# A GNN layer's edge sums: two masked sums per partition on VectorE in place of eight bf16 matmuls on TensorE

## The chip, the cores and the metric

The kernel runs on one core of one Trainium2 chip. The core has five engines that run on their own and meet at semaphores: TensorE (PE, matrix products), VectorE (DVE), ScalarE (ACT), GpSimd (POOL, which here issues the gathers) and SyncE (SP, which here issues loads and stores). SBUF is the working memory of 128 partitions; matrix products land in PSUM. The metric is the device time of one execution in microseconds (us), as a median of several runs.

## What is computed

One layer of a graph network with 6250 nodes, 206250 edges and 64 features. The edges are sorted by destination node `dst`; every node has one loop edge and on average 33 edges.

```python
h = jnp.maximum(_layernorm(x, axis=-1), 0.0)

def _L0_gnn_ref(x, edge_index, edge_attr, W1, b1, W2, b2):
    src = edge_index[0]
    dst = edge_index[1]
    msg = jax.nn.relu(x[src] + edge_attr)
    agg = jax.ops.segment_sum(msg, dst, num_segments=x.shape[0])
    h = x + agg
    h = jax.nn.relu(h @ W1 + b1)
    return h @ W2 + b2

x = x + _L0_gnn_ref(h, edge_index, edge_attr_64, ...)
```

So: normalise the node rows, gather one row per edge, add the edge's own row, relu, sum per destination node, then two 64x64 layers.

## The kernel before

**Tiling.** The edges go in `NG` = 201 groups of 1024 (`GE`: 128 partitions with `G` = 8 consecutive edges each) and a tail group of 426 edges in `CT` = 4 columns. Nodes go in `NB` = 12 blocks of 512 and a rest of 106. Since the edges are sorted, a group touches a window of consecutive nodes; the kernel sums each group into a window of `W` = 64 nodes that begins at the group's first node.

**Start** (lines 72 to 226). Node rows are loaded, normalised (`ln_head`, `ln_rows`), written to DRAM as `h_rows` for the gathers, and turned by TensorE (`ln_turn`; ScalarE copies them) into `z`, which holds the sums, one column per node. The first `RAW` = 4 groups gather raw `x` rows, since `h_rows` isn't written yet, and are normalised per edge (`norm_edges`). Then `slot` is made: for each edge the place of its node in its group's window, from `base`, the window starts, which a one-row matmul spreads over the partitions (lines 214 to 226).

**The edge loop** (lines 342 to 355), for each group g:
- `load` (134): SP loads the edge rows `ea`, and POOL issues eight indirect DMAs (130), one for each column of 128 rows, into `xg`. Both have `LOOK` = 12 buffers, so POOL may be up to 12 groups ahead of the instruction that reads a buffer last.
- `window_sum` (287): a one-hot `oh` of `slot` against `wslots`, which lies in PSUM (294); `full = xg + ea` into PSUM (299); relu and a split of the fp32 messages into three bf16 parts, ScalarE and VectorE by turns (301 to 305); eight matmuls that add the three parts of all edges into `agg`, 64 nodes by 3 x 64 (308).
- `turn(g-1)` (275): VectorE adds the three parts of the group before into `agg_rows` (278), and TensorE transposes them (280).
- `sum_into_z(g-2)` (283): VectorE adds the transpose into `z` at a column read from a register (285). `LAG` = 2 is this distance.
- `blocks_behind(g-2)` (335): once all edges of a block of nodes are in (`READY`), `hidden` (312) makes relu(W1 z + b1), and at the next group `result` (321) makes the second product, adds `x` and stores.

At g = 8, `find_left` (239) marks edges that no window holds, and `flag`; at g = 9, `b2` is added to `x_sb` by 13 additions (353, 355). After the loop a register reads `flag`; if any edge is left, a second loop over all groups and windows repairs the result (379 to 399). With these inputs it has nothing to do.

**Order.** The schedule is written out by hand: each engine takes its instructions in the order of the program, and waits in it. POOL and SP wait for nothing but buffers and, at the stores, for SP's data, so they run ahead of the others.

Of the kernel before, what the change touches and what calls it, by code (L numbers as in the profile page):

```python
# [18 lines left out]
P = 128  # L19
G = 8  # L20
GE = P * G
# [15 lines left out]
LOOK = 12  # L37
LAG = 2
RV = 8
RAW = 4  # L40
# [5 lines left out]
def kernel(  # L46
# [143 lines left out]
    def ln_turn(c, h):  # L190
        for b in range(XC if c < NB else 1):
            pt = psum.tile([D, R, P], F32, name="big", bufs=1)
            n0 = (c + b) * P * R
            if c < NB:
                for r in range(R):
                    nc.tensor.transpose(pt[:, r, :], h[:, b * R + r, :], ident)  # L196
                nc.scalar.copy(z[:, n0:n0 + P * R].rearrange("d (p r) -> d r p", r=R), pt)  # L197
            else:
                nc.tensor.transpose(pt[:, 0, :TN], h[:TN, 0, :], ident[:TN, :TN])
                nc.scalar.copy(z[:, n0:N], pt[:, 0, :TN])  # L200

    heads, rows = [], []
# [6 lines left out]
    rows.append(ln_rows(*heads[-1]))  # L209
    ln_turn(*rows[-2])  # L210
# [3 lines left out]
    base = const.tile([1, NG + 1], F32, name="base")  # L214
    nc.vector.tensor_copy(base, dst_sb[0:1, 0:C + 1:G])
    pb = psum.tile([P, R * D], F32, name="out", bufs=1)
    nc.tensor.matmul(pb[:, :NG + 1], ones[0:1, :], base, start=True, stop=True)
# [10 lines left out]

    def combine(xg, ea, n):
        nc.vector.tensor_tensor(xg[:, :n], xg[:, :n], ea[:, :n], ALU.add)  # L230
        msg = work.tile([P, G, D], F32, name="msg")
        nc.scalar.activation(msg[:, :n], xg[:, :n], AF.Relu)
        return msg
# [3 lines left out]
    flag = const.tile([1, 1], I32, name="flag")  # L237

    def find_left():
        nc.vector.tensor_scalar(left, slot, 1.0, None, op0=ALU.is_lt)  # L240
        nc.vector.scalar_tensor_tensor(left, slot, float(W), left, op0=ALU.is_gt, op1=ALU.add)
# [5 lines left out]
        nc.tensor.matmul(pf[0:1, 0:1], most, ones[:, 0:1], start=True, stop=True)  # L247

# [23 lines left out]

    turned = {}

    def turn(g):
        pa = aggs.pop(g)
        rows = work.tile([W, D], F32, name="agg_rows")
        nc.vector.tensor_reduce(rows, pa.rearrange("w t d -> w d t"), AX.X, ALU.add)  # L278
        pt = psum.tile([D, W], F32, name="turned", bufs=1)
        nc.tensor.transpose(pt, rows, ident[:W, :W])  # L280
        turned[g] = pt

    def sum_into_z(g):
        at = window_start(g)
        nc.vector.tensor_tensor(z[:, ds(at, W)], z[:, ds(at, W)], turned.pop(g), ALU.add)  # L285

    def window_sum(g):
        n = G if g < NG else CT
        cols = cols_of(g)
        ea, xg = loaded[g] if g < RAW else load(g)  # L290
        if g < RAW:
            norm_edges(xg)
        oh = work.tile([P, G, W], BF16, name="oh")
        nc.vector.tensor_tensor(  # L294
            oh[:, :n], slot[:, cols].unsqueeze(2).to_broadcast([P, n, W]),
            wslots.unsqueeze(1).to_broadcast([P, n, W]), ALU.is_equal)

        full = psum.tile([P, G, D], F32, name="full", bufs=2)
        nc.vector.tensor_tensor(full[:, :n], xg[:, :n], ea[:, :n], ALU.add)  # L299
        parts = work.tile([P, G, 3, D], BF16, name="parts")  # L300
        nc.scalar.activation(parts[:, :n, 0, :], full[:, :n], AF.Relu)  # L301
        nc.vector.scalar_tensor_tensor(full[:, :n], full[:, :n], 0.0, parts[:, :n, 0, :],  # L302
                                       op0=ALU.max, op1=ALU.subtract)
        nc.scalar.copy(parts[:, :n, 1, :], full[:, :n])  # L304
        nc.vector.tensor_tensor(parts[:, :n, 2, :], full[:, :n], parts[:, :n, 1, :], ALU.subtract)  # L305
        pa = psum.tile([W, 3, D], F32, name="agg", bufs=2)
        for j in range(n):
            nc.tensor.matmul(pa, oh[:, j, :], parts[:, j], start=(j == 0), stop=(j == n - 1))  # L308
        aggs[g] = pa


    def hidden(c):
        n0 = c * P * R
        p, r = (P, R) if c < NB else (TN, 1)
        p1 = psum.tile([D, P * R], F32, name="big", bufs=1)
# [5 lines left out]
    def result(c, h1):  # L321
# [3 lines left out]
        for k in range(r):  # L325
            nc.tensor.matmul(p2[:p, k * D:(k + 1) * D], h1[:, k, :p], w2_sb, start=True, stop=True)  # L326
        o = work.tile([P, R, D], F32, name="o")
# [5 lines left out]
    hid = {}  # L333

    def blocks_behind(g):
        for c in sorted(hid):
            result(c, hid.pop(c))
        for c in range(NB):
            if READY[c] == g:
                hid[c] = hidden(c)  # L340

    for g in range(NG + 1):
        window_sum(g)
        if g >= 1:
            turn(g - 1)
# [5 lines left out]
        if g == 9:  # L351
# [4 lines left out]
    sum_into_z(NG + 1 - LAG)  # L356
    blocks_behind(NG + 1 - LAG)
    turn(NG)
    for g in range(NG + 2 - LAG, NG + 1):
        sum_into_z(g)  # L360
        blocks_behind(g)
    hid[NB] = hidden(NB)
    for c in sorted(hid):
        result(c, hid.pop(c))


    def all_windows(msg, lf, n):
        for w in range(0, N, WB):
# [3 lines left out]
            pw = psum.tile([D, WB], F32, name="big", bufs=1)  # L372
# [7 lines left out]
    with tc.If(any_left > 0):  # L380
# [17 lines left out]
        for c in range(NB + 1):  # L398
            result(c, hidden(c))
# [39 lines left out]
```

## Time and profile before

| | us |
|---|---|
| median of 6 runs | 2361.32 |
| lowest, highest | 2356.5, 2387.14 |
| the profiled execution, timed | 2357.45 |
| its span in the profile | 2355.7 |
| POOL busy, 1612 gathers | 1589.7 |
| first gather starts, last one ends | 4.6, 2287.1 |
| VectorE busy | 668.8 |
| TensorE busy (ends modelled) | 414.0 |
| ScalarE busy | 267.9 |

The page gives busy time of each engine, a chain of waits followed back from the end, and groups of instructions with the line of the kernel: so many, their busy time, the mean of one in ns, the idle time of the engine before them and what ended it ("issue": nothing that the profile shows; "remote": a semaphore whose setter isn't known). The timeline lists instructions in order of time: start in us, duration, engine, line, and in brackets the idle time before. Durations of one group's instructions on VectorE: L294 0.67, L299 0.69, L302 0.70, L305 0.69, L278 0.34, L285 0.21 us.

### The profile page before, as it was taken

The page shows a single profiled execution, that of the slowest core. Times are in us where ns is not written, and L with a number is a line of the kernel's source. Part 1 is how long each engine was busy: PE and PEld are TensorE (multiplying, and loading weights), DVE is VectorE, ACT ScalarE, POOL GpSimd, SP SyncE. Part 2 cuts the span into 40 slices and gives each one's busy share as a digit, 9 for nine tenths or more (in the row PEclk, how much of TensorE's full clock was granted, in tenths as well). Part 3 has the DMA queues.
Part 4 walks back from the last instruction along what each step waited for, and adds up shares of the span by engine and source line. Part 5 has one row for each costly group of instructions (what it writes and reads, how often), then busy time and mean ns, then how long its engine had stood idle before and what let it go on. Part 6 is the DMA issues. An engine that isn't in the chain of part 4 may idle for free.

```text
span 2355.7 us, 9645 instructions
## 1 busy us (share of the span) xinstructions
PE 414.0 (18%) x1991; PEld 287.0 (12%) x1991; DVE 668.8 (28%) x1321; ACT 267.9 (11%) x450; POOL 1590.9 (68%) x1619
## 2 busy tenths in 40 slices
PE   1101320031122012030122013001212011120303
PEld 1000210020011011020111012001111011110202
DVE  3313621141242133150243124112324023131515
ACT  2100210010011011020011011001111011010202
POOL 7775777567667757577567757766666676766760
DMA  5111131012113103111203103110311130130310
GB/s 160 39 35 35 28 94 31 21 45 76 26 22 99 26 19 94 30 24 51 69 23 94 35 19 94 31 23 21 92 32 23 24 96 21 26 98 21 91 23 4
DMA packets 87525, 112.95 MB, mean 48 GB/s; under 512 B 30948, under 2 KB 35684, under 8 KB 87460
## 3 DMA queue, kind: packets, MB, share of 16 engines
q0 software_dynamic: 51584, 52.93, 10.0%
q1 hardware_dynamic: 34628, 57.65, 7.3%
q10 hardware_dynamic: 1248, 1.70, 0.2%
q14 instruction: 48, 0.39, 0.1%
q8 instruction: 17, 0.28, 0.0%
HBM read 108.96 MB, written 3.20 MB: 48 GB/s over the span
## 4 chain that ended last, share of the span: by engine, by line
another core or an unknown queue 33%; issue 31%; DVE 13%; POOL 11%; ACT 5%; DVEq 3%; DMA 2%; PE 2%; ACTq 0%; SPq 0%; POOLq 0%
POOL xg L130 11%; DVE full L302 4%; DVE full L299 3%; ACT parts L301 3%; ACT parts L304 2%; DVE parts L305 2%; DVE oh L294 2%; DVEq L265 2%; DMA xg<-h_rows,src_sb 1%; DVEq L299 1%; PE agg L308 1%; DVE agg_rows L278 1%; DVE z L285 1%; DMA x_sb<-in_x_dram 0%
## 5 line engine op out<-in xcount | busy, mean ns | idle before, releaser
L130 POOL DMA_INDIRECT xg<-h_rows,src_sb x1580 | 1557.2, 986 | 683.3 <-issue 456.3
L308 PE MATMUL agg<-parts,oh 128*64 128x192 bf16 x1612 | 299.7, 367 | 903.9 <-DVE parts L305 504.8
L308 PEld LDWEIGHTS <-oh 128*64 128x64 bf16 x1612 | 229.8, 167 | 958.3 <-DVE parts L305 543.9
L301 ACT ACTIVATE parts<-full 128x512 bf16<-128x512 f32 x202 | 120.2, 595 | 1696.7 <-DVE full L299 1254.6
L278 DVE TENSOR_REDUCE agg_rows<-agg 64x64 f32<-64x192 f32 x202 | 69.4, 343 | 825.6 <-remote 669.4
L280 PE MATMUL turned<-ident,agg_rows 64*64 64x64 f32 x202 | 63.1, 312 | 962.3 <-issue 493.4
L302 DVE SCALAR_TENSOR_TENSOR full<-full,parts 128x512 f32<-128x512 f32 x202 | 141.1, 699 | 229.1 <-ACT parts L301 109.8
L305 DVE TENSOR_TENSOR parts<-full,parts 128x512 bf16<-128x512 f32 x202 | 139.4, 690 | 131.5 <-ACT parts L304 83.9
L299 DVE TENSOR_TENSOR full<-xg,ea 128x512 f32<-128x512 f32 x202 | 138.5, 686 | 64.7 <-DMA ea<-in_edge_attr_dram 31.1
L280 PEld LDWEIGHTS turned<-ident,agg_rows 64*64 64x64 f32 x202 | 25.4, 126 | 1024.4 <-issue 538.4
L304 ACT CAST parts<-full 128x512 bf16<-128x512 f32 x202 | 118.2, 585 | 154.6 <-DVE full L302 113.2
L294 DVE TENSOR_TENSOR oh<-slot,wslots 128x512 bf16<-128x512 f32 x202 | 135.7, 672 | 0.0
L285 DVE TENSOR_TENSOR z<-z,turned 64x64 f32 x202 | 42.0, 208 | 227.6 <-remote 131.9
L328 DVE TENSOR_TENSOR o<-out,x_sb 128x256 f32<-128x256 f32 (+1 forms) x13 | 5.3, 410 | 127.3 <-remote 62.2
L130 POOL DMA_INDIRECT xg<-in_x_dram,src_sb x32 | 32.6, 1017 | 12.3 <-issue 9.5
L316 PE MATMUL big<-z,w_sb 64*64 64x512 f32 (+1 forms) x26 | 24.2, 1032 | 0.3 <-DVE z L285 0.3
L326 PE MATMUL out<-w_sb,h 64*128 64x64 f32 (+1 forms) x98 | 23.6, 418 | 1.2 <-ACT h L318 1.2
L326 PEld LDWEIGHTS out<-w_sb,h 64*128 64x128 f32 (+1 forms) x98 | 22.3, 329 | 3.2 <-ACT h L318 3.2
L318 ACT ACTIVATE h<-big,b_sb 64x512 f32<-64x512 f32 (+1 forms) x13 | 8.5, 656 | 123.3 <-issue 48.1
L196 PE MATMUL big<-ident,ln_h 128*64 128x128 f32 x48 | 12.7, 420 | 52.6 <-issue 21.0
L197 ACT COPY z<-big 64x512 f32<-64x512 f32 x12 | 12.6, 1050 | 39.7 <-issue 30.6
L196 PEld LDWEIGHTS big<-ident,ln_h 128*64 128x64 f32 x48 | 6.4, 158 | 58.5 <-issue 41.7
(52 smaller groups left out, 64.2 us busy)
## 6 DMA issues: line engine op xcount, KB each, us to landing
ea<-in_edge_attr_dram SPq DMA_DIRECT2D x201, 256.0 KB
xg<-h_rows,src_sb POOLq DMA_INDIRECT x1580
x_sb<-in_x_dram SPq DMA_DIRECT2D x4, 384.0 KB
h_rows<-ln_h SPq DMA_DIRECT2D x4, 384.0 KB
out_dram<-o SPq DMA_DIRECT2D x12, 128.0 KB
dst_sb<-in_dst_main_dram ACTq DMA_DIRECT2D x1, 804.0 KB
src_sb<-in_src_main_dram ACTq DMA_DIRECT2D x1, 788.0 KB
xg<-in_x_dram,src_sb POOLq DMA_INDIRECT x32
```

The lines of the kernel that those rows point to most:

```text
L130: nc.gpsimd.indirect_dma_start(out=xg[:, j, :], out_offset=None, in_=rows[:, :], in_offset=bass.IndirectOffsetOnAxis(ap=idx[:, j:j + 1], a ...
L265: _, vals = nc.values_load_multi_w_load_instructions(dst_sb[0:1, g * G:(g + n - 1) * G + 1:G], engines=(DVE,), min_val=0, max_val=N - 1)
L278: nc.vector.tensor_reduce(rows, pa.rearrange("w t d -> w d t"), AX.X, ALU.add)
L280: nc.tensor.transpose(pt, rows, ident[:W, :W])
L285: nc.vector.tensor_tensor(z[:, ds(at, W)], z[:, ds(at, W)], turned.pop(g), ALU.add)
L294: nc.vector.tensor_tensor(oh[:, :n], slot[:, cols].unsqueeze(2).to_broadcast([P, n, W]), wslots.unsqueeze(1).to_broadcast([P, n, W]), ALU. ...
L299: nc.vector.tensor_tensor(full[:, :n], xg[:, :n], ea[:, :n], ALU.add)
L301: nc.scalar.activation(parts[:, :n, 0, :], full[:, :n], AF.Relu)
L302: nc.vector.scalar_tensor_tensor(full[:, :n], full[:, :n], 0.0, parts[:, :n, 0, :], op0=ALU.max, op1=ALU.subtract)
L304: nc.scalar.copy(parts[:, :n, 1, :], full[:, :n])
L305: nc.vector.tensor_tensor(parts[:, :n, 2, :], full[:, :n], parts[:, :n, 1, :], ALU.subtract)
L308: nc.tensor.matmul(pa, oh[:, j, :], parts[:, j], start=(j == 0), stop=(j == n - 1))
```

## The change

Within a partition, the eight consecutive edges of a group belong to at most two nodes here, a first and a last one. `cut` makes, once, two masks of all edges: `of_run[0]`, equal to the partition's first slot, and `of_run[1]`, equal to its last slot but not its first; `run_slot` keeps the two slots (a third for the tail's fourth column). For each group, VectorE then adds `ea` to `xg` in place in SBUF, and for each mask takes max(., 0) times the mask into `msg` and sums its eight edges into a column block of `sums`, 128 x 64 fp32. TensorE multiplies `sums` with a one-hot of the partition's slots, now fp32, made for `OB` = 4 groups at a time: two fp32 matmuls a group, which give node columns directly, so `agg_rows`, the transpose and the split are gone. ScalarE has no part in it any more.

The sum into `z` follows six groups behind (`LAG`), the buffers are 14 (`LOOK`), five groups gather raw rows (`RAW`), the window starts are spread before the last two `ln_turn`, the flag is judged at g = 14, `b2` is added at g = 15, and a block's second product and its store come two and four groups after its first product. An edge in a third node of its partition would count as left.

```diff
+RUNS = 2
-LOOK = 12
-LAG = 2
+LOOK = 14
+LAG = 6
+OB = 4
-RAW = 4
+RAW = 5
...
+    def cut(g, n, cols, k):
+        sv = slot[:, cols].rearrange("p (g j) -> p g j", j=k)
+        first, last = [t[:, cols].rearrange("p (g j) -> p g j", j=k) for t in of_run]
+        nc.vector.tensor_tensor(first, sv, sv[:, :, 0:1].to_broadcast([P, n, k]), ALU.is_equal)
+        nc.vector.tensor_tensor(last, sv, sv[:, :, k - 1:k].to_broadcast([P, n, k]), ALU.is_equal)
+        nc.vector.tensor_tensor(last, last, first, ALU.is_gt)
+        nc.vector.tensor_copy(run_slot[:, g:g + n, 0], sv[:, :, 0])
+        nc.vector.tensor_copy(run_slot[:, g:g + n, 1], sv[:, :, k - 1])
+    cut(0, NG, slice(0, C), G)
+    cut(NG, 1, slice(C, C + TJ), TJ)
...
     def find_left():
-        nc.vector.tensor_scalar(left, slot, 1.0, None, op0=ALU.is_lt)
-        nc.vector.scalar_tensor_tensor(left, slot, float(W), left, op0=ALU.is_gt, op1=ALU.add)
+        nc.vector.tensor_tensor(left, of_run[0], of_run[1], ALU.add)
+        nc.vector.tensor_scalar(left, left, 0.5, None, op0=ALU.is_lt)
+        nc.vector.scalar_tensor_tensor(left, slot, 1.0, left, op0=ALU.is_lt, op1=ALU.max)
+        nc.vector.scalar_tensor_tensor(left, slot, float(W), left, op0=ALU.is_gt, op1=ALU.max)
         nc.vector.scalar_tensor_tensor(left, dst_sb, 1.0, left, op0=ALU.add, op1=ALU.mult)
...
     def sum_into_z(g):
         at = window_start(g)
-        nc.vector.tensor_tensor(z[:, ds(at, W)], z[:, ds(at, W)], turned.pop(g), ALU.add)
+        nc.vector.tensor_tensor(z[:, ds(at, W)], z[:, ds(at, W)], aggs.pop(g), ALU.add)
+    def one_hot(g, n, runs):
+        oh = work.tile([P, OB, RUNS + 1, W], F32, name="oh", bufs=4)
+        nc.vector.tensor_tensor(
+            oh[:, :n, :runs], run_slot[:, g:g + n, :runs].unsqueeze(3).to_broadcast([P, n, runs, W]),
+            wslots.unsqueeze(1).unsqueeze(1).to_broadcast([P, n, runs, W]), ALU.is_equal)
...
     def window_sum(g):
-        nc.vector.tensor_tensor(full[:, :n], xg[:, :n], ea[:, :n], ALU.add)
-        ...
-        for j in range(n):
-            nc.tensor.matmul(pa, oh[:, j, :], parts[:, j], start=(j == 0), stop=(j == n - 1))
+        sums = work.tile([P, RUNS + 1, D], F32, name="sums", bufs=LAG + 2)
+        nc.vector.tensor_tensor(xg[:, :m], xg[:, :m], ea[:, :m], ALU.add)
+        for k in range(RUNS):
+            msg = work.tile([P, G, D], F32, name="msg")
+            nc.vector.scalar_tensor_tensor(
+                msg[:, :n], xg[:, :n], 0.0, of_run[k][:, col:col + n].unsqueeze(2).to_broadcast([P, n, D]),
+                op0=ALU.max, op1=ALU.mult)
+            nc.vector.tensor_reduce(sums[:, k], msg[:, :n].rearrange("p j d -> p d j"), AX.X, ALU.add)
+        ...
+        for k in range(runs):
+            nc.tensor.matmul(pa, sums[:, k], oh[:, k], start=(k == 0), stop=(k == runs - 1))
...
     def blocks_behind(g):
+        for c in sorted(res):
+            if READY[c] + 4 <= g:
+                store(c, res.pop(c))
         for c in sorted(hid):
-            result(c, hid.pop(c))
+            if READY[c] + 2 <= g and not res:
+                res[c] = result(c, hid.pop(c))
```

## The prediction

> **What bounds the kernel now.** I read the costliest groups first, then the list of waits, then three stretches of the timeline. The page's busy times and the shares of its chain:
>
> ```profile
> PE 414.0 (18%) x1991; PEld 287.0 (12%) x1991; DVE 668.8 (28%) x1321; ACT 267.9 (11%) x450; POOL 1590.9 (68%) x1619
> ...
> another core or an unknown queue 33%; issue 31%; DVE 13%; POOL 11%; ACT 5%; DVEq 3%; DMA 2%; PE 2%; ACTq 0%; SPq 0%; POOLq 0%
> ```
>
> and two groups from the list by shape (busy us, mean ns of one | idle before, and what ended it):
>
> ```profile
> L130 POOL DMA_INDIRECT xg<-h_rows,src_sb x1580 | 1557.2, 986 | 683.3 <-issue 456.3 <-DVE full L299 209.3 <-DMA xg<-h_rows,src_sb 17.7
> ...
> L278 DVE TENSOR_REDUCE agg_rows<-agg 64x64 f32<-64x192 f32 x202 | 69.4, 343 | 825.6 <-remote 669.4 <-issue 141.0 <-PE agg L308 15.2
> ```
>
> POOL issues 1612 gathers, eight a group, one every 1.25 us (median 0.947 us, then 0.30 us of issue). That alone is 2012 us. The rest of POOL's row: 209.3 us in 26 waits for L299, the reader that frees an xg buffer. So two things matter: how fast POOL goes, and how often VectorE is 12 groups behind.
>
> Why VectorE is behind: L278 waits 669.4 us, 61 times, on a semaphore whose setter the profile can't name. In the timeline it is TensorE's:
>
> ```profile
> 930.32 0.69 DVE L305 TENSOR_TENSOR parts<-full,parts 128x512 bf16<-128x512 f32 x1 [0.65 <-ACT parts L304]
> ...
> 931.07 1.49 PE L308 MATMUL agg<-parts,oh 128*64 128x192 bf16 x8 [3.66 <-issue]
> ...
> 947.83 0.35 DVE L278 TENSOR_REDUCE agg_rows<-agg 64x64 f32<-64x192 f32 x1 [16.81 <-remote]
> ...
> 951.33 0.21 DVE L285 TENSOR_TENSOR z<-z,turned 64x64 f32 x1 [3.15 <-remote]
> ```
>
> L278 at 947.83 reads the group before, whose matmuls the records end at 917.96: the result arrives 30 us late, the transpose's after another 3.5 us. In such episodes a group takes 25.2 us; outside, 4.38 us. They begin at a block's `hidden` and end only a few us after POOL has run dry of buffers. Why TensorE's results come late there I can't tell.
>
> What slows POOL itself. Timeline again (start, us, engine, line):
>
> ```profile
> 1008.35 1.58 POOL L130 DMA_INDIRECT xg<-h_rows,src_sb  x1 [0.30 <-issue]
> 1008.42 0.68 DVE L299 TENSOR_TENSOR full<-xg,ea 128x512 f32<-128x512 f32 x1
> ...
> 1009.85 0.70 DVE L302 SCALAR_TENSOR_TENSOR full<-full,parts 128x512 f32<-128x512 f32 x1 [0.75 <-ACT parts L301]
> 1010.23 0.94 POOL L130 DMA_INDIRECT xg<-h_rows,src_sb  x1 [0.30 <-issue]
> ```
>
> A gather that starts beside L299 takes 0.63 us more; one beside L302 nothing. L299 reads two tensors in SBUF, L302 one in PSUM. Over all gathers: L299 running about 0.1 us after the gather's start stretches it to L299's end plus 0.82 us. Two other stretches:
>
> ```profile
> 97.80 0.69 DVE L157 SCALAR_TENSOR_TENSOR xg<-xg,ln_v 128x512 f32<-128x512 f32 x1
> 98.14 1.18 POOL L130 DMA_INDIRECT xg<-h_rows,src_sb  x1 [0.30 <-issue]
> ```
>
> ```profile
> 239.50 4.10 DVE L353 TENSOR_TENSOR x_sb<-x_sb,b_sb 128x256 f32<-128x256 f32 x12
> 240.19 4.37 POOL L130 DMA_INDIRECT xg<-h_rows,src_sb  x1 [0.30 <-issue]
> ```
>
> L157 has the form of the change's mask multiply, and blocks too. Thirteen independent adds in a row let no gather through (3.42 us lost). But between L240, L241 and L242, each reading what the one before wrote, there is a gap of 35 ns, and one gather gets through each time. Gathers starting beside reductions of SBUF (L148, L154) take 0.95 us.
>
> **The sum today.** 1612 x 0.947 + 1586 ordinary gaps of 0.305 (483.4) + 209.3 waits + 65.2 stretched gathers (55.2 in 117 by L299, 10 by one-time work) + 4.6 before the first = 2289, against 2287.1 read; then 68.6 of tail, mostly the backlog of 12 groups at 4.38 us. Span 2355.7, timed 2357.45, 1.75 around it; the median of six is 3.9 above that (0.16%).
>
> **Part by part.**
> *TensorE and LAG.* Per group 8 bf16 matmuls and a transpose become two fp32 matmuls of 64 columns; agg_rows is gone; z is summed six groups behind, some 62 us at POOL's pace, with 14 buffers in place of 12. In the late state a 64x64 fp32 product is 2.45 to 4.3 us (the waits at L285), so a pair 5 to 8.6; a block's `hidden` and `result` add some 40 us per 16.5 groups, 2.4 each (`hidden` held ScalarE 11.4 us at 1056, the outputs 25 at 1086). 7.4 to 11 us a group against POOL's 10.2: TensorE just keeps up, and what it loses, 20 groups of slack take. Behind a late z sum queue the next group's add and the mask multiplies, and POOL's buffers behind those. Waits W: from 0 to today's 209.3; I take 10.
> *ScalarE.* Relu and cast (238 us) go; they were beside POOL's work: 0.
> *VectorE.* Per group now: add 0.69, two mask multiplies 0.70 (L157), two reductions 0.69 (L154), a quarter of a one-hot 0.17 (L294), z 0.20: 3.8 us against 3.3 and POOL's 10.2, so time on VectorE costs 0. The new reductions step 256 bytes through SBUF; L278, with that step in PSUM, took 343 ns for 192, so I keep 0.69; at four times that VectorE is at 8 us and still covered, and at five it would bind. SBUF — State Buffer of the Trainium skill (The DMA port swizzle) says an access that crosses a 16-byte line pays a penalty; no row here has such a step in SBUF, and the sum is the same either way.
> *The lock, B.* Three two-SBUF-input operations a group instead of one. The add starts when the last gather has landed, 2.06 us after its start by the DMA packets, so some 0.87 us into the next gather; the following one reads 0.49 us into the add and waits 0.18. Its successor comes 1.25 later, beside the first reduction; the next, after the second multiply: 0.18 a group, 36 us. Averaged over all offsets the same steps give 0.46 (92 us), the worst offset 0.90 (181 us). VectorE will not always be waiting for the landing; I take 0.27, what L299 costs per group today: 55 us. SBUF — State Buffer (Who interferes with whom) says that of two such instructions the second fully blocks, which speaks against this change: two more of 0.70 in full on 201 groups would put 281 us on top of today's 55; L302's 0.94 and the 117 of 202 stretched say POOL needs the port for a moment, so I price by those. The same section says tensor_tensor was not seen to stall a DMA; 1.58 us differs.
> *Set-up.* `cut` has three two-input passes over 128x1612 and `find_left` two more; as L241 cost a gather 0.62, 3.1; the copies 0.3 and the fifth raw group's L150 and L157 0.6: 4 in all. The extra VectorE work itself, some 13 us (five passes of 1.84 and about 4 for the fifth group's norm), is spent while POOL has 14 groups of buffers: 0. Moving `base` past the last transposes ends a 38.7 us wait on VectorE at L219, but group 0 still waits for ScalarE's copies to 77 us: 0.
> *SP.* `store` waits in SP's queue ahead of the edge loads of later groups, as now (L299 waited 31.1 us in ten such places); VectorE caught up in a few groups, POOL didn't notice: 0.
> *Tail T.* From the last group's L299 to the end today: 16.0; with the landing, 18; to 69 if a backlog stands. `hidden(11)` and the outputs, late, add some 10: 30.
>
> New span: 2287.1 - 209.3 - 55.2 = 2022.6; the 26 waits become ordinary gaps, +7.9 = 2030.5. +4 +55 +10 +30 = 2129.5; with 1.75 around it 2131; towards the median, 2132.
> Its own range: 2030.5+4+36+0+18 = 2089 to 2030.5+4+181+30+69 = 2315.
>
> **The rivals.**
> 1. *The pair is held from the add through the first multiply*, without the gap that L240 to L242 show, as with L353: at 0.49 a gather waits 0.90 and the next 0.23 at the second multiply; 1.13 a group, 227 us: 2302 + 1.75 = 2304. For: L353. Against: L241/L242 depend on each other as these do.
> 2. *Slower: POOL locked out from the add to the end of the second multiply*, the reduction between included: 2.87 us held, 2.38 lost a group, 478 us, about 2555. Slower from B over 281 us, 1.40 a group; by over 1% from 1.52. For: three of five operations hold the port. Against: 0.94 and 0.95 beside L148 and L154.
> 3. *TensorE stays the bound*: fp32 products over 128 rows take longer in the late state than 64x64 shows, episodes and buffer waits remain: W 209, T 69: 2030.5+4+55+209+69 = 2367.5, 2369 timed; 2406 with B at 92.
> 4. *The repair loop runs*, if three nodes meet in one partition's eight edges: thousands of us. A node has 33 edges on average (206250/6250), and three would need one with at most six.
>
> **How the numbers follow.** This measurement can tell about 1% from no change. Forecast 0.74; rival 1 0.07; rival 2 0.06; rival 3 0.12, half within 1%, half slower; rival 4 0.01. Faster: 0.74 + 0.07 = 0.81; same 0.06; slower 0.13. The range takes in the forecast's ends and most of rival 1: 2085 to 2320.
>
> **What would show it.** Right: POOL's idle before L130 falls to about 490 with no wait above a few us; L278's kind of wait moves to the z sum and is short; gathers beside the add and the multiplies are stretched, their sum between 36 and 181 over the set-up's 14; the last gather ends near 2100. Wrong: mean gather above 1.05 us with the gap unchanged (rivals 1 and 2; 2 if gathers beside the reduction are long), or waits of POOL for the second multiply of 5 us and more (3).

## The result and the profile after

| | us |
|---|---|
| predicted, range | 2132, 2085 to 2320 |
| after: median of 20 runs (lowest, highest) | 2323.61 (2280.27, 2333.68) |
| before: median of 46 runs (lowest, highest) | 2371.44 (2347.76, 2389.48) |
| ratio after/before, 95% interval | 0.9722, 0.9687 to 0.9756 |
| profiled execution after: timed, span | 2299.31, 2297.5 |

The change made the kernel 2.8% faster: the two medians are 48 us apart, where 229 us were forecast, and the time lies 4 us above the range. Busy times, chain and costliest groups after (line engine op, busy us, mean ns of one | idle us before, releaser):

```profile
PE 252.3 (11%) x987; PEld 149.3 (6%) x987; DVE 923.2 (40%) x1395; ACT 31.4 (1%) x48; POOL 1696.2 (74%) x1619
...
POOL 54%; issue 20%; another core or an unknown queue 11%; DVE 7%; DMA 5%; DVEq 2%; PE 0%; POOLq 0%; ACT 0%; SPq 0%; ACTq 0%
...
L132 POOL DMA_INDIRECT xg<-h_rows,src_sb x1572 | 1655.1, 1053 | 535.0 <-issue 463.9
L341 DVE TENSOR_REDUCE sums<-msg 128x64 f32<-128x512 f32 x404 | 407.2, 1008 | 16.7 <-DVE msg L338 3.0
...
L334 DVE TENSOR_TENSOR xg<-xg,ea 128x512 f32<-128x512 f32 x202 | 138.4, 685 | 425.3 <-DMA xg<-h_rows,src_sb 317.7
L311 DVE TENSOR_TENSOR z<-z,agg 64x64 f32 x202 | 41.6, 206 | 661.4 <-remote 484.3
```

POOL (GpSimd) now leads the chain, as forecast: its idle time falls from 683.3 to 535.0 us. But its mean gather grew from 986 to 1053 ns, a reduction takes 1008 ns where 0.69 us were assumed, and the z sum still waits 661.4 us for something. The last gather ends at 2247.7 (forecast about 2100), and 49.8 us follow it. Two stretches of the timeline show what holds the gathers (start, us, engine, line; idle before in brackets):

```profile
1023.61 0.98 POOL L132 DMA_INDIRECT xg<-h_rows,src_sb  x1 [0.30 <-issue]
1023.92 0.69 DVE L334 TENSOR_TENSOR xg<-xg,ea 128x512 f32<-128x512 f32 x1 [2.77 <-DMA xg<-h_rows,src_sb]
1024.65 0.69 DVE L338 SCALAR_TENSOR_TENSOR msg<-xg,run 128x512 f32<-128x512 f32 x1
1024.89 1.27 POOL L132 DMA_INDIRECT xg<-h_rows,src_sb  x1 [0.30 <-issue]
...
1026.31 0.68 DVE L338 SCALAR_TENSOR_TENSOR msg<-xg,run 128x512 f32<-128x512 f32 x1
...
1026.47 1.33 POOL L132 DMA_INDIRECT xg<-h_rows,src_sb  x1 [0.30 <-issue]
...
1043.11 1.08 POOL L132 DMA_INDIRECT xg<-h_rows,src_sb  x1 [0.31 <-issue]
1044.49 1.09 POOL L132 DMA_INDIRECT xg<-h_rows,src_sb  x1 [0.30 <-issue]
...
1048.43 0.21 DVE L311 TENSOR_TENSOR z<-z,agg 64x64 f32 x1 [20.39 <-remote]
```

First, a gather that starts while a mask multiply (L338) runs takes 1.27 or 1.33 us in place of 0.95: the lock that the prediction priced. Second, with VectorE idle for 20 us, the gathers take 1.08 or 1.09, and their starts lie some 1.40 us apart (1.38 in these lines), which no step of the prediction foresaw.

Over all gathers, the time above 0.946 us is 172.3 us. Sorted by what VectorE runs about 0.1 us after a gather's start (another instant moves a few gathers and an us or two), it is 66.9 beside the multiplies (206 of 215 gathers), 24.5 beside the add, 8.8 beside the reductions, 56.0 with VectorE idle (376 of 1035), 16 beside the rest. Five waits of POOL for a buffer, of 1.4 to 21.3 us, add 49 us.

### The profile page after: what moved, and what is told of

Read it like the earlier page. It is cut to its first block, busy times and chain, and to the rows that moved or that the text cites. A ratio compares the mean times of both kernels' runs of the same rounds, so it can differ in the third digit from the quotient of the medians.

```text
span 2297.5 us, 7096 instructions
## 1 busy us (share of the span) xinstructions
PE 252.3 (11%) x987; PEld 149.3 (6%) x987; DVE 923.2 (40%) x1395; ACT 31.4 (1%) x48; POOL 1696.2 (74%) x1619
## 4 chain that ended last, share of the span: by engine, by line
POOL 54%; issue 20%; another core or an unknown queue 11%; DVE 7%; DMA 5%; DVEq 2%; PE 0%; POOLq 0%; ACT 0%; SPq 0%; ACTq 0%
POOL xg L132 54%; DMA xg<-h_rows,src_sb 5%; DVE sums L341 3%; DVE msg L338 3%; DVE xg L334 1%; DVEq L299 1%; DVEq L334 1%; DVE z L311 0%; DVE oh L315 0%; DMA src_sb<-in_src_main_dram 0%; POOLq L132 0%; DMA ea<-in_edge_attr_dram 0%; PE out L366 0%; PE big L356 0%
## 5 line engine op out<-in xcount | busy, mean ns | idle before, releaser
L132 POOL DMA_INDIRECT xg<-h_rows,src_sb x1572 | 1655.1, 1053 | 535.0 <-issue 463.9
L341 DVE TENSOR_REDUCE sums<-msg 128x64 f32<-128x512 f32 x404 | 407.2, 1008 | 16.7 <-DVE msg L338 3.0
L348 PE MATMUL agg<-oh,sums 128*64 128x64 f32 x810 | 192.1, 341 | 1931.9 <-DVE sums L341 1032.3
L334 DVE TENSOR_TENSOR xg<-xg,ea 128x512 f32<-128x512 f32 x202 | 138.4, 685 | 425.3 <-DMA xg<-h_rows,src_sb 317.7
L311 DVE TENSOR_TENSOR z<-z,agg 64x64 f32 x202 | 41.6, 206 | 661.4 <-remote 484.3
L338 DVE SCALAR_TENSOR_TENSOR msg<-xg,run 128x512 f32<-128x512 f32 x404 | 277.5, 687 | 9.3 <-remote 2.5
L348 PEld LDWEIGHTS agg<-oh,sums 128*64 128x64 f32 x810 | 116.5, 205 | 2023.9 <-DVE sums L341 1081.5
L132 POOL DMA_INDIRECT xg<-in_x_dram,src_sb x40 | 39.9, 997 | 15.8 <-issue 11.9
L315 DVE TENSOR_TENSOR oh<-run_slot,wslots 128x512 f32<-128x512 f32 (+2 forms) x52 | 34.2, 658 | 0.0
```

The lines of the kernel that those rows point to most:

```text
L132: nc.gpsimd.indirect_dma_start(out=xg[:, j, :], out_offset=None, in_=rows[:, :], in_offset=bass.IndirectOffsetOnAxis(ap=idx[:, j:j + 1], a ...
L311: nc.vector.tensor_tensor(z[:, ds(at, W)], z[:, ds(at, W)], aggs.pop(g), ALU.add)
L315: nc.vector.tensor_tensor(oh[:, :n, :runs], run_slot[:, g:g + n, :runs].unsqueeze(3).to_broadcast([P, n, runs, W]), wslots.unsqueeze(1).un ...
L334: nc.vector.tensor_tensor(xg[:, :m], xg[:, :m], ea[:, :m], ALU.add)
L338: nc.vector.scalar_tensor_tensor(msg[:, :n], xg[:, :n], 0.0, of_run[k][:, col:col + n].unsqueeze(2).to_broadcast([P, n, D]), op0=ALU.max, ...
L341: nc.vector.tensor_reduce(sums[:, k], msg[:, :n].rearrange("p j d -> p d j"), AX.X, ALU.add)
```

## The experiments

Kernels of one set ran on one chip and share the runs of the kernel before. The sets fell into two kinds that had not been expected, and nothing below can be read without this table:

| set, chip | kernel before, median us | kernels |
|---|---|---|
| recorded | 2371 | the change: 0.972 |
| 1, chip 4 | 2050.6 | e1 to e4 |
| 2, chip 0 | 2365.1 | e5 to e7 |
| 3, chip 1 | 2397.0 | e8 to e10 |
| 4, chip 5 | 2055.3 | e11 to e14 |
| 5, chip 5 | 2055.5 | e15, e16 |
| 6, chip 10 | 2361.2 | e17 |
| 7, chip 0 | 2054.3 | e18 |

The same kernel took 2050 to 2055 us in four sets and 2361 to 2397 in the others. Expectations written before set 7 speak of chips that have the slow spells; chip 0 shows both kinds, so it is not the chip. I call the sets of 2361 and more "with spells", for what their traces show, the others "clean". The first four expectations were written in the belief that the kernel before takes 2370.

### What is the lock worth? e1, e2, e11

**e1: the sum to PSUM**, so that the multiplies read one tensor of SBUF only.

```diff
-        nc.vector.tensor_tensor(xg[:, :m], xg[:, :m], ea[:, :m], ALU.add)
+        full = psum.tile([P, G, D], F32, name="full", bufs=1)
+        nc.vector.tensor_tensor(full[:, :m], xg[:, :m], ea[:, :m], ALU.add)
         ...
-                msg[:, :n], xg[:, :n], 0.0, of_run[k]...
+                msg[:, :n], full[:, :n], 0.0, of_run[k]...
```

> The sum of gathered and edge rows goes to PSUM, so the two mask multiplies have one SBUF input each and only the add has two. Theory (the lock adds to POOL's time one to one): the stretch of gathers that meet a multiply, 66.9 us in the changed kernel, goes to 0 and the last gather ends some 65 us earlier; time 2235 to 2250 where the changed kernel is at about 2310. Rival (TensorE's late results set the pace and POOL's gain is waited away): the stretch goes, but POOL's waits for buffers grow from 52 us by as much, and the time moves by less than 20.

Set 1: 2050.77 us, 1.0001 of before (0.9991 to 1.0010). The gathers and the multiplies of that run:

```profile
L132 POOL DMA_INDIRECT xg<-h_rows,src_sb x1572 | 1494.6, 951 | 479.1 <-issue 433.3
...
L339 DVE SCALAR_TENSOR_TENSOR msg<-full,run 128x512 f32<-128x512 f32 x404 | 276.2, 684 | 7.0
...
L311 DVE TENSOR_TENSOR z<-z,agg 64x64 f32 x202 | 41.2, 204 | 85.1 <-issue 82.8
```

A gather takes 951 ns, and nothing but the ordinary 0.30 us lies between two. Beside the multiplies none of 341 gathers is stretched, beside the reductions none of 248, beside the add 12 of 34 (3.3 us). z waits 85.1 us instead of 661.4. The last gather ends at 2033.8: this is POOL's own pace, so there was nothing to gain over the kernel before in this set. The stretch by the multiplies is gone, as both sides expected; which of them is right about the time can't be read here, since z's sum isn't late in this set.

**e2: ScalarE copies z's block**, and the hidden layer's multiply reads the copy, so that z's next sum need not wait for that read (`h1` has two buffers, to make room).

```diff
-        nc.tensor.matmul(p1[:, :p * r], w1_sb, z[:, n0:n0 + p * r], start=True, stop=True)
+        zc = work.tile([D, P * R], F32, name="zc", bufs=1)
+        nc.scalar.copy(zc[:, :p * r], z[:, n0:n0 + p * r])
+        nc.tensor.matmul(p1[:, :p * r], w1_sb, zc[:, :p * r], start=True, stop=True)
```

> ScalarE copies a finished block of z and hidden reads the copy; h1 has two buffers in place of four. Theory (the sum into z that follows a block's hidden waits for TensorE's late read of z, 21 to 55 us in seven of twelve blocks): these waits vanish, the sum of waits before the z sum falls from 661 to under 400, POOL's buffer waits from 52 to under 15, the tail from 50 to under 35; time 2245 to 2270. Rival (the waits are TensorE's lateness itself and move to the next bank's first group): sum of z waits stays above 550 and the time moves by less than 15.

Set 1: 2165.51, 1.0559 of before (1.0542 to 1.0577). z waits 84.2 us, so what the copy was to end was not there. 380 of 383 gathers beside the multiplies are stretched, by 114.2 us in all; the distance to e1 is 114.7 us. In this set the change costs what its multiplies hold up, and no wait hides it.

**e11: the changed kernel as it is** (no edit). In e5 and e8 below it had run with spells; set 4 was clean.

> The changed kernel as it is, the measure for the three that follow. On chips 0 and 1 it took 2305 to 2324 us at 0.968 to 0.971 of the kernel before; on a chip like 4, where it hasn't run, 2160 to 2172 us against 2050.6.

2153.54, 1.0479 of before (1.0462 to 1.0496): the same change, 4.8% slower. Page and timeline:

```profile
L132 POOL DMA_INDIRECT xg<-h_rows,src_sb x1572 | 1595.8, 1015 | 479.1 <-issue 424.3
...
L341 DVE TENSOR_REDUCE sums<-msg 128x64 f32<-128x512 f32 x404 | 407.2, 1008 | 13.9
...
L311 DVE TENSOR_TENSOR z<-z,agg 64x64 f32 x202 | 41.4, 205 | 85.0 <-issue 82.7
```

```profile
1006.88 0.95 POOL L132 DMA_INDIRECT xg<-h_rows,src_sb  x1 [0.31 <-issue]
1006.91 0.70 DVE L334 TENSOR_TENSOR xg<-xg,ea 128x512 f32<-128x512 f32 x1 [6.22 <-DMA xg<-h_rows,src_sb]
1007.64 0.69 DVE L338 SCALAR_TENSOR_TENSOR msg<-xg,run 128x512 f32<-128x512 f32 x1
1008.13 1.01 POOL L132 DMA_INDIRECT xg<-h_rows,src_sb  x1 [0.30 <-DMA xg<-h_rows,src_sb]
1008.36 1.01 DVE L341 TENSOR_REDUCE sums<-msg 128x64 f32<-128x512 f32 x1
1009.29 0.68 DVE L338 SCALAR_TENSOR_TENSOR msg<-xg,run 128x512 f32<-128x512 f32 x1
...
1009.45 1.34 POOL L132 DMA_INDIRECT xg<-h_rows,src_sb  x1 [0.30 <-issue]
```

The add begins 0.03 us after the start of a gather and costs nothing: in this run it begins within 0.25 us after a gather's start in 181 groups, always after a wait, and stretches none of these gathers (in the kernel before, where L299 mostly followed another instruction at once, such a start did stretch them). The first multiply's end catches the next gather (1.01), the second multiply the one after (1.34): 0.06 + 0.39 us lost a group. Over the run: 99.3 us in 374 of 377 gathers beside the multiplies, 3.3 beside the add, 0 beside the reductions (28 gathers), under 1 with VectorE idle.

### The reduction's size: e7

The products are written with a node's eight edges side by side, so that the reduction reads them in order.

```diff
-            msg = work.tile([P, G, D], F32, name="msg")
+            msg = work.tile([P, D, G], F32, name="msg")
             ...
-                msg[:, :n], xg[:, :n], 0.0, ...
+                msg[:, :, :n].rearrange("p d j -> p j d"), xg[:, :n], 0.0, ...
-            nc.vector.tensor_reduce(sums[:, k], msg[:, :n].rearrange("p j d -> p d j"), AX.X, ALU.add)
+            nc.vector.tensor_reduce(sums[:, k], msg[:, :, :n], AX.X, ALU.add)
```

> The changed kernel, with the products written with a node's 8 edges side by side, so that each reduction reads its 8 numbers next to each other. Tests the size of the reduction: 0.69 us in my sum, 1.01 in the trace of the changed kernel, where the second multiply starts 2.38 us after the addition instead of 2.1. If the reduction falls to 0.69 and the multiplies stay at 0.69, the second multiply ends 2.78 us after the addition's start instead of 3.07: it then overlaps the third gather's read by 0.13 instead of 0.39 us, the lock costs 0.2 to 0.3 us a group instead of 0.57, and the kernel takes 2090 to 2115 us where the changed one takes 2165 (or 40 to 60 us less than the changed one where TensorE is late, if lock and lateness add). Rival: the strided write makes the multiplies as long as the reductions were (1.0 us), the lock is held longer, and it takes 2200 to 2300. Rival: the start of the addition slides until the loss is the same, and nothing changes (2160 to 2170).

Set 2, with spells: 2312.63, 0.9827 of before (0.9748 to 0.9906), against 0.9705 (0.9615 to 0.9795) for the changed kernel there; the intervals overlap, so the times don't tell the two apart. The profile does: the first rival's mechanism held, the multiplies became as long as the reductions had been (its 2200 to 2300 us was missed):

```profile
L338 DVE SCALAR_TENSOR_TENSOR msg<-xg,run 128x512 f32<-128x512 f32 x404 | 432.3, 1070 | 6.9
...
L341 DVE TENSOR_REDUCE sums<-msg 128x64 f32<-128x512 f32 x404 | 276.4, 684 | 13.8
```

The price of the 256-byte step moved from the read of the reduction (1008 to 684 ns) to the write of the multiply (687 to 1070 ns), which holds the gathers: 113.6 us beside the multiplies, 69.1 in e5. So the step's price is shown; that a reduction of 0.69 us with short multiplies would halve the lock was not tried.

### With and without spells: e5, e6, e8

No edits: the changed kernel twice more, and the kernel before.

> The changed kernel as it is, timed against the kernel before once more. In the last four runs the kernel before took 2050.6 us instead of 2371, and no TensorE result came late (the wait of z's sum ahead of its additions was 84 to 85 us in all, instead of 661). If the lock theory holds, the change is worth what its lock costs wherever TensorE is not late: the kernel with z's copy had 114.2 us of stretched gathers under the multiplies and took 2165.5, and the changed kernel differs from it by a copy that nobody waits for there, so 2160 to 2172 us against 2050.6, slower by 5 to 6%. If instead that copy (or its fewer buffers) cost the 115 us, the changed kernel takes 2050 to 2090. Where the kernel before takes about 2370 us again, so does the changed one about 2320, and the gain comes and goes with the late results of TensorE.

> The kernel before as it is, for its profile. Where it takes about 2050 us, the 26 waits of GpSimd for buffers (209.3 us in the profile shown) are gone, the gathers stretched with VectorE idle or adding are few (under 15 us in all, instead of 65.2), the gathers' mean is 950 to 955 ns instead of 986, and the tail is under 20 us instead of 68.6. If instead GpSimd itself is faster there, the gap of 0.305 us or the undisturbed 0.947 us of a gather is shorter. Where it takes about 2370 us, its groups wait for TensorE in spells of 25 us, as before.

> The changed kernel as it is, beside the two that follow. So far the kernel before took 2361 to 2371 us on one chip (0), where the changed one took 2305 to 2324, and 2050.6 us on another (4), where the changed one hasn't run. On a chip like 4 the changed kernel should be slower than before: its lock costs there what the kernel with z's copy showed (114.2 us under the multiplies), so 2160 to 2172 us. Rival: the copy of z or its fewer buffers made that, and it takes 2050 to 2090. On chip 0 it repeats 2.9% faster (ratio 0.960 to 0.980).

The changed kernel took 2304.87 (0.9705, 0.9615 to 0.9795) in set 2 and 2324.42 (0.9676, 0.9614 to 0.9737) in set 3; e6 was one execution of 2385.63. Both sets had spells, so e5 and e8 repeat the recorded result, and the profile of a clean kernel before is still missing.

What a spell is can be read from the kernel before in the recorded set. The chain of waits there, in order of time (start, us; DVEq is VectorE's own queue of register and semaphore instructions):

```profile
1300.60 0.18 DVEq L265
...
1300.87 0.18 DVEq L265
...
1304.08 0.71 DVEq L285
1304.80 0.69 issue
1305.49 0.71 DVEq L299
1306.20 0.69 issue
1306.89 0.70 DVEq L299
```

Up to 1301.7 us there is a pair of them every 0.28 us (0.18 and 0.02 us long; the lines show the longer one). From 1304 on each takes 0.70 us, and 0.70 us pass before most of them: 1.40 us from start to start. In the changed kernel 322 of 1429 of VectorE's register and semaphore instructions last 0.64 to 0.76 us in the recorded set; in the same kernel in the clean set 4 (e11) none of 1429. POOL's gathers, 1.40 us apart, follow the same beat: 395 of 1611 steps, against 49 in e11.

TensorE's records don't show it, since their ends are modelled; the semaphore that TensorE raises does. In the changed kernel each of a group's two multiplies is two weight loads and two matmuls, 4 instructions, and 121 of 323 intervals between two updates are 5.6 us = 4 x 1.40; in e11 not one. A group is 8 instructions, 11.2 us. In the kernel before it is 9 weight loads and 9 matmuls: 18 x 1.40 = 25.2 us, which is the group time that the prediction read in its "episodes". That the count of instructions sets the time is so far an inference from these three products.

One more sign separates the sets, in the last lines of the pages, where a DMA's time from issue to landing stands when it can be read. First the recorded set, then e11, the same kernel:

```profile
xg<-h_rows,src_sb POOLq DMA_INDIRECT x1572
```

```profile
xg<-h_rows,src_sb POOLq DMA_INDIRECT x1572, 2.4
```

With spells the landing time is missing, because most records of semaphore updates are: the recorded set's trace of the changed kernel holds 5754, e11's 31684. It is so throughout: 3842 to 7541 in the nine traces with spells, 31358 to 31690 in the ten clean ones that gather. The instructions themselves are all there (7096 in both). So what slows the engines comes together with a loss of the profiler's records; which causes which, or whether both have a third cause, isn't shown. It also means that the intervals between TensorE's updates are read from 324 updates, where e11 has 409.

### Which edit helps where there are spells? e9, e10

> The changed kernel with the sum xg + ea written to PSUM, so that the multiplies read one input from SBUF only and no longer hold the gathers. On a chip like 4 it repeats 2050.8. On chip 0, if the lock adds to TensorE's lateness: the multiplies' 69 us and the reductions' 8 us of stretched gathers go, the addition's 27 and the 53 us of gathers stretched with VectorE idle stay, so 2304.9 - 77 = 2228, in 2210 to 2250. Rival: TensorE's late results set the time there and GpSimd's faster gathers only wait longer for buffers: 2285 to 2310, with more than 100 us of waits over 1 us (52 us in the changed kernel).

> The sum in PSUM and z's block copied by ScalarE before the hidden layer's multiply, both. On a chip like 4: 2050 to 2053, nothing to gain. On chip 0, against the kernel with the sum in PSUM alone: if z's sum waits long after a block because its write must follow the hidden layer's late read of z, the copy ends that: its waits of 20 to 55 us at the eight blocks go, the waits for buffers of some 52 us and part of the tail of 50 with them, 40 to 90 us less. Rival: what comes late is TensorE as a whole, the copy waits for nothing less, and the two are within 15 us of each other.

e9 is e1's edit, e10 both e1's and e2's. Set 3: 2343.88 (0.9767, 0.9724 to 0.9811) and 2333.77 (0.9742, 0.9705 to 0.9780), beside 0.9676 of the changed kernel. Taking the lock away gained nothing here; e9's page and its list of waits:

```profile
L132 POOL DMA_INDIRECT xg<-h_rows,src_sb x1572 | 1605.1, 1021 | 591.3 <-issue 490.5
...
L311 DVE TENSOR_TENSOR z<-z,agg 64x64 f32 x202 | 41.5, 205 | 783.9 <-remote 465.0
```

```profile
POOL xg L132 <- DVE full L335: 70.6, 9, 24.7
```

The mean gather falls from 1049 (e8) to 1021 ns, but POOL's waits over 1 us grow from 67 to 110 us and the tail from 76 to 92. From group 60 on VectorE is mostly 8 to 14 groups behind the gathers, waiting in its queue for late z sums; a faster POOL only fills its buffers sooner. So the rival of e9's expectation held in kind (over 100 us of waits; its 2285 to 2310 us were meant for chip 0). e10 is within 11 us of e9, as its rival said: z's waits fell from 783.9 to 621.1 us with the copy, but most of them have another reason than the read of z by the hidden layer.

### The count of instructions: e3, e12 to e18

```diff
-        oh = work.tile([P, OB, RUNS + 1, W], F32, name="oh", bufs=4)
+        oh = work.tile([P, OB, RUNS + 1, W], BF16, name="oh", bufs=4)
-        sums = work.tile([P, RUNS + 1, D], F32, name="sums", bufs=LAG + 2)
+        sums = work.tile([P, RUNS + 1, D], BF16, name="sums", bufs=LAG + 2)
```

With bf16 columns (e3, e12, e15, e18) a multiply is one weight load and one matmul: 4 instructions a group for TensorE in place of 8.

> The sums and the one-hot are bf16, so that the pair of products is bf16 in place of fp32; the output carries the sums' rounding to bf16. Theory A (TensorE's fp32 products, late as they are, stretch gathers by 0.15 us while VectorE is idle, and take 5.6 us a pair): the 56 us of stretch with VectorE idle falls under 10, the pair under 2.5, z waits under 300; time 2210 to 2240. Rival B (a waiting z sum in VectorE's queue stretches them): stretch per idle gather stays, time above 2280.

> The changed kernel with the column sums and the one-hot matrices in bf16: the same multiply takes one weight load and one matmul instead of two each, so TensorE is sent 4 instructions a group instead of 8. New theory: on chips 0 and 1 there are spells in which an engine's instructions leave its queue one per 1.40 us (the semaphore that TensorE raises comes every 5.60 us, 4 instructions, in 121 of 323 intervals of the changed kernel, in none of the kernel with z's copy on chip 4), and what made 'TensorE late' is its count of instructions: 18 a group before (25.2 us), 8 after (11.2 us, more than GpSimd's 10.0). With 4 it needs 5.6 us, keeps up, and z's waits, the waits for buffers (55 us) and the tail (50 to 76 us) go: 2190 to 2240 on chip 0 or 1, 0.92 to 0.945 of before, where the changed kernel has 0.97. Rival: VectorE's own queue sets the pace in the spells (5 semaphore and register instructions a group and 16 more for each 8 groups, 9.8 us a group), and bf16 gains under 1%. On a chip like 4 it repeats 2165.

> The changed kernel with bf16 columns and one-hot again, for a chip with the spells. There the theory of TensorE's instruction count expects 0.92 to 0.945 of before (the changed kernel: 0.968 and 0.971) and z's waits under 300 us instead of 650 to 760; the rival of VectorE's own queue expects 0.96 to 0.975. On a chip without the spells it repeats 1.048 to 1.056.

> The changed kernel with bf16 columns and one-hot, for a chip with the spells. The kernel with all three edits came to 0.959 there, with z's waits at 28.5 us and GpSimd's gathers themselves at 11.2 us a group (8 instructions by 1.40). If TensorE's count alone had made z wait: z's waits under 200 us here too, and 0.955 to 0.965, the lock hidden in GpSimd's own slow issue. If VectorE's bounds checks had their part: 0.963 to 0.975, with z's waits of 200 to 500 us. If the lock adds to GpSimd's slow issue: 0.975 to 1.0 with short z waits. On a chip without the spells it repeats 1.047 to 1.056.

All four met clean sets: 1.0560, 1.0475, 1.0473 and 1.0553 of before (each interval within 0.002). TensorE isn't late there, and halving its instructions changes nothing: e12 and e11 are 0.7 us apart. Alone, this edit never met spells, so it tests none of the theories in these four expectations.

e13 drops the bounds check of the addresses that VectorE loads, one instruction of its queue a group:

```diff
-                dst_sb[0:1, g * G:(g + n - 1) * G + 1:G], engines=(DVE,), min_val=0, max_val=N - 1)
+                dst_sb[0:1, g * G:(g + n - 1) * G + 1:G], engines=(DVE,), min_val=0, max_val=N - 1,
+                skip_runtime_bounds_check_because="node numbers of the edges lie in 0..N-1")
```

> The changed kernel without the bounds check of the 8 addresses that VectorE loads for z's sums (one instruction of VectorE's queue a group less, of 7). If VectorE's queue sets the pace in the spells, its group falls from 9.8 to 8.4 us there, some 60 of 202 groups have it slow, and 40 to 85 us go on chip 0 or 1 (2230 to 2280). If TensorE's count of instructions does, nothing to 15 us. On a chip like 4: 2160 to 2172, as the changed kernel.

Set 4, clean: 2155.38, 1.0483 (1.0466 to 1.0501), as the changed kernel. For spells it says nothing.

e14, e16 and e17 join the three edits: bf16 columns, no bounds check, the sum in PSUM.

> All three: bf16 columns, no bounds check, and the sum xg + ea in PSUM so that the multiplies don't hold the gathers. On chip 0 or 1, if both theories hold (few instructions keep up in the spells, and then the lock's 77 us count in full): 2100 to 2165, 0.885 to 0.915 of before. If the lock's share is still hidden there, within 1% of the bf16 kernel. On a chip like 4: 2050 to 2053, equal to before.

> bf16 columns, no bounds check, the sum in PSUM, again for a chip with the spells: 0.885 to 0.915 of before if few instructions keep up and the lock's 77 us then count; within 1% of the bf16 kernel if they stay hidden; 0.97 to 0.98, as the kernel with the sum in PSUM alone, if neither instruction count matters. On a chip without the spells it repeats 0.998.

> bf16 columns, no bounds check, the sum in PSUM, once more for a chip with the spells. There it differs from the kernel with the sum in PSUM alone (0.977 of before) by the instructions sent to TensorE (4 a group instead of 8) and by VectorE's bounds checks only. If the count of instructions made TensorE and VectorE late: 0.885 to 0.915 of before, z's waits under 300 us instead of 784. If it did not: 0.965 to 0.98. On a chip without the spells it repeats 0.998 to 0.999.

Clean: 2052.24 (0.9984, 0.9975 to 0.9994) and 2052.91 (0.9990, 0.9980 to 1.0000). With spells, in set 6: 2269.16, 0.9592 (0.9516 to 0.9667), between the two numbers expected. Page and timeline of e17:

```profile
L133 POOL DMA_INDIRECT xg<-h_rows,src_sb x1572 | 1652.4, 1051 | 527.1 <-issue 497.2
...
L313 DVE TENSOR_TENSOR z<-z,agg 64x64 f32 x202 | 41.3, 205 | 28.5 <-issue 26.2
```

```profile
1247.57 1.10 POOL L133 DMA_INDIRECT xg<-h_rows,src_sb  x1 [0.30 <-issue]
1248.97 1.10 POOL L133 DMA_INDIRECT xg<-h_rows,src_sb  x1 [0.30 <-issue]
1250.38 1.10 POOL L133 DMA_INDIRECT xg<-h_rows,src_sb  x1 [0.30 <-issue]
```

The size was wrong. The mechanism was right as far as the late z sum goes: z waits 28.5 us (e9: 783.9), as much as in the clean sets without the bounds check (28.5 in e13), POOL has a single wait over 1 us, of 2.8, and the tail is 30 (e9: 92). VectorE still had a spell. None of its 1025 register and semaphore instructions is slow, but from 116 to 685 us its other instructions are held back. Many start on the beat of 1.40 us, and a group takes 7.7 to 9.8 us, most often 8.4 (6 x 1.40):

```profile
L341 DVE SCALAR_TENSOR_TENSOR msg<-full,run 128x512 f32<-128x512 f32 x404 | 276.3, 684 | 159.2 <-remote 121.9
```

```profile
209.18 0.69 DVE L341 SCALAR_TENSOR_TENSOR msg<-full,run 128x512 f32<-128x512 f32 x1 [3.26 <-remote]
210.58 1.01 DVE L344 TENSOR_REDUCE sums<-msg 128x64 bf16<-128x512 f32 x1 [0.71 <-issue]
```

In the clean e14 these multiplies wait 6.9 us. At this pace VectorE keeps up with POOL, which has a beat of its own: single gathers start mostly 1.25 to 2.1 us apart, but the mean is 1.38, a group of 8 takes 11.2 us (8 x 1.40), and the last gather ends at 2237.1 of a span of 2267.5. Whether TensorE's halved count, VectorE's missing checks or another kind of spell on chip 10 did it is open, since neither edit alone met spells and the kernel with the sum in PSUM alone didn't run in this set. In set 4 this version beats the changed kernel by 101 us; in its one set with spells it beats the kernel before by 4%, where the changed kernel gained about 3% in other sets. The column sums have bf16 precision in it.

### TensorE without POOL: e4

```diff
+            o = (g * 25) % (N - GE)
+            nc.sync.dma_start(out=xg..., in_=h_rows[o:o + P * n, :]...)
+        for _ in range(9):
+            nc.vector.tensor_copy(pad..., wslots...)
```

SyncE loads consecutive rows in place of the gathered ones, so the output isn't the reference's, and nine copies a group fill VectorE.

> From the sixth group on xg is loaded by SP from consecutive rows, so POOL is silent, and nine PSUM copies of 0.69 us a group keep VectorE at about 10.5 us a group; the result is of other edges. Theory C (results come late whenever TensorE has little to do): a pair still takes about 5.6 us, z waits and waits after a block remain. Rival D (POOL's gathers make them late): a pair under 1.5 us, no wait before a z sum above 2 us. Time about 2200 either way.

One execution of 2353.21 us in set 1, VectorE busy 2158 us. TensorE's updates came at once, but in this set they did so beside POOL's gathers too (e1, e2): the question was not reached.

## Why the prediction was wrong

Several steps failed. First by its own sum, in the recorded set: from the forecast span of 2129.5 to the measured 2297.5 are 168 us.

1. **"TensorE just keeps up, and what it loses, 20 groups of slack take" (W 10)** failed. In a spell TensorE's group is 11.2 us by its count of instructions, with a block's products on top, at POOL's 10.2; VectorE stood behind late z sums, as the same paragraph had warned. 49 us of waits where 10 were taken: +39. The tail T, 30 predicted, was 49.8: +20.
2. **"POOL issues 1612 gathers, one every 1.25 us"** was taken as fixed. 56 us went to gathers 1.40 us apart with VectorE idle. The profile of before has 3 such steps; that POOL meets them only once it has stopped waiting fits this, but isn't shown.
3. **B, the lock, 55 us** was mis-sized. Clean (e11) it is 102.6 us, 0.51 a group where 0.27 was taken. Beside the add and the multiplies the recorded run shows 91.4 (+36), where slow steps of POOL may be among them, and 8.8 more beside the reductions (+9), which stretch no gather in e11. Two inputs were off: the reduction is 1.008 us, not 0.69, and the add starts 2.59 us after the last gather's start (median of e11), not 2.06, so near a gather's start and not 0.87 us into it. "The sum is the same either way", said of the reduction, was wrong by the timeline of e11: VectorE has the time, but the second multiply moves to where it meets the next gather; no run has short reductions beside short multiplies to test it. The mean over all offsets, 92 us, which was named and not taken, is nearer.

These are 39 + 20 + 56 + 36 + 9 = 160 of 168 us. The rest is small: the set-up was some 7 us for 4. They say where POOL's time went, not what each is worth alone: e9 took the lock away in a set with spells, and the waits and the tail grew instead.

The largest step is none of these terms. All cases, the rivals too, set out from the kernel before at 2357 us, with 209.3 us of buffer waits for the change to win. Those waits belong to the spells ("Why TensorE's results come late there I can't tell"). In the clean sets the kernel before takes 2050 to 2055 us, which leaves no room for them: it is at POOL's pace, only the lock is left, and the change costs 4.8% (4.7 to 5.6% with e2, e3, e12, e13, e15 and e18, which keep the lock); that its new kernel at 2153.5 lies within the range is a coincidence of two errors.

What was right: POOL becomes the bound; its floor (2030.5 forecast for the last gather, 2033.8 in e1); only the multiplies and the add hold gathers, the reductions don't, against rival 2; the pair isn't held through, against rival 1 (all ten gathers that the add stretches in e11 end 0.8 us after the add, as a single hold gives); the repair loop stays out. Rival 3 was nearest in mechanism, with its waits at a quarter of its price; the sign set for rivals 1 and 2, a mean gather above 1.05 us, showed too (1.053), but for the reasons 2 and 3 above. A slip without effect: reductions of five times 0.69 us would bring VectorE to 9.3 us a group, which does not yet bind at 10.2.

The Trainium skill's page "SBUF — State Buffer" (section "Who interferes with whom") says that a VectorE instruction with two SBUF inputs contends with a GpSimd instruction that reads SBUF, and that one with at most one SBUF input does not, outside certain two-port modes. e11 against e1 agrees: 374 of 377 gathers beside the multiplies stretched, then none of 341. The price, 0.25 us a multiply of 0.69 (99.3 us in 404), is the runs' alone; it lies well below the 281 us that the prediction worked out for two multiplies that block in full.

## What to carry to other kernels

When a profile shows a wait whose setter it can't name, and a beat that no instruction's duration explains (here 1.40 us), ask whether the kernel or the day makes it: a change that lives off such a wait may gain 3% in one set of runs and lose 5% in the next, so time before and after beside each other, more than once. An operation that has time to spare on its own engine can still have a price if its length decides where the next operation meets another engine. Moving one operand to PSUM took some 100 us off GpSimd in the clean sets (1595.8 to 1494.6 us of gathers, e11 to e1) with the multiplies as long as before (685 and 684 ns); with spells it gained nothing (e9).

## What the runs showed of the hardware

- **Spells of slow issue.** In four of eight sets instructions of VectorE, TensorE's multiplies (by its semaphore) and GpSimd's gathers leave 1.40 us apart for stretches of tens to hundreds of us, one engine at normal pace beside another in a spell (e9 at 1313 to 1350 us: POOL 1.25 us, VectorE's queue 1.40). The cost fits the count of instructions: 5.6 us for 4, 11.2 for 8 and 25.2 for 18 of them are 1.40 each. The kernel before loses 311 us to it (2361 to 2050), the changed one 170 (2324 to 2154), the one with few instructions 217 (2269 to 2052), this last one nearly all in POOL. What sets it off stays open: chip 0 had it in set 2 and not in set 7, and the granted clock (0.51 in some executions, 1.0 in others) takes both values in both kinds. Traces with spells lack three quarters or more of the records of semaphore updates that the clean ones have.
- The Trainium skill's page "NOTIFIC — the notification-queue block" (section "7.1 Overflow: three behaviours, one of which stalls the engine") says that the block through which engines write their records can hold them back. The loss of records in the sets with spells makes the recording a suspect, but every execution here was recorded, so no run shows whether that is the cause, or what the kernels take unrecorded.
- **A 256-byte step in SBUF** costs a pass over 128x512 fp32 some 0.32 us as a reduction's read (1008 against 684 ns) and 0.38 as a multiply's write (1070 against 687).
